# Graph attention stack: the one-head layer's division by the softmax sum, on ScalarE in place of VectorE

## The chip, the cores and the metric

The kernel runs on one core of one Trainium2 chip. The metric is the device time of one execution in microseconds, as the median of several. The core has a matrix engine (TensorE, "PE" in the profile; its weight loads are "PEld"), VectorE ("DVE"), ScalarE ("ACT"), GpSimd ("POOL") and SyncE ("SP", which here only issues DMAs). Each engine works through its own instructions in order; between engines there are semaphores.

## The reference

A stack of four graph attention layers over N = 3327 nodes with 512 features and one sparse 0/1 adjacency matrix (symmetric, with self loops). The layers have 8, 4, 1 and 8 heads. The third, with one head, is the one that matters here:

```
h  = relu(layernorm(x))            # before every layer
h  = h @ W                         # 3327 x 512
e  = leaky_relu(s1[:, None] + s2[None, :], 0.2)      # s1 = h @ a1, s2 = h @ a2
e  = where(adj > 0, e, -9e15)
h' = softmax(e, axis=1) @ h
x  = x + elu(h')
```

The softmax is computed as a sum of exp(e) times rows of h, and a division by the sum of exp(e). That last product of a 128 x 512 tile with one reciprocal per row is what this document calls a mean.

## The kernel before, in words

The nodes are padded to 3328 and cut into 26 tiles of 128 rows, sorted by the number of neighbours. The first layer's preparation turns the adjacency matrix into lists of neighbours. Then a layer treats its tiles in two ways. Tiles with few neighbours (17 of 26 in the third layer) work from lists: `Tile.fetch` gathers a neighbour's row for each of the 128 nodes by an indirect DMA on GpSimd (L834), four neighbours to a group and seven groups ahead; `scored` adds the scores on VectorE (L887, L889) and takes their exponential on ScalarE (L890); `group` multiplies and adds the rows. With one head, `group` does this on VectorE alone: L909 writes the first product into the PSUM tile `bank`, L911 adds the others to it. Tiles with many neighbours (9 in the third layer, in three sets of three) are dense: `Wholes` takes all 26 tiles of rows one after the other, ScalarE makes weights r (L1116), VectorE masks them (em, L1123), TensorE multiplies them with the rows into three PSUM banks `whole` (L1150); GpSimd and VectorE add up the sums (L1136, L1142).

Both sorts run interleaved. The program is written in steps, one group of a list tile to a step, and the order on TensorE, VectorE, ScalarE and GpSimd is that of the program; SP's order is found by a scheduler. Within a step there are places, in this order: "first" (loads, mask product and the next weights, products of the dense tiles), the scores and exponentials of the next step, "scored", the group itself, and "last". A tile's end is spread over later steps by `ends`: `bent` (ScalarE, L944 and L946, for the elu), `added` (VectorE, L952 and L958), `centre` (ScalarE, L966 and L969), `root` (L974 on VectorE, L431 on GpSimd), `turn` (TensorE, L450), `cut` (ScalarE, hT, L457), `project` (TensorE, pv, L468) and `rows` (ScalarE, v, L475, then a DMA to the table of the next layer).

`Tile.finish` puts `divisors` (L926 to L928) and, with one head, `means` (L934) into "last" of the tile's last step. `Wholes.means` (L1161 and L1077 three times) stands three steps after a set's last row tile. In this layer the PSUM pool "o" has one buffer for each name, so the `bank` of the next list tile is the same memory:

```python
            pools = {"o": pool("ps_o", 1 if whole else 2, **psum)}
            ...
                pools.update(w=pool("ps_w", 3, **psum), e=pool("epool", 1))
```

`whole` has three buffers, one for each tile of a set, which the next set takes over. The means are written to SBUF, to parts of `low`: two in turn for list tiles, three for dense ones.

Of the kernel before, what the change touches and what calls it, by code (L numbers as in the profile page):

```python
# [14 lines left out]
AF = mybir.ActivationFunctionType  # L15
OP = mybir.AluOpType
# [779 lines left out]
def tile_gat_lists(ctx: ExitStack, tc: tile.TileContext, x, adj, ws, avs, out, ident, half, slots, L, low, spare, tabx, tabs):  # L796
# [7 lines left out]
    nc = tc.nc  # L804
# [40 lines left out]
    class Tile:  # L845
# [84 lines left out]
        def means(self):  # L930
            H, den = HEADS[self.l], self.den
            if H == 1:
                self.y = next(ys)
                nc.vector.tensor_scalar(self.y, self.po, den[:, 0:1], None, OP.mult)  # L934
                return
            self.y = self.po
            y = self.y.rearrange("p (h d) -> p h d", h=H)
            nc.vector.tensor_tensor(y, y, den[:, :H].unsqueeze(2).to_broadcast([P, H, F // H]), OP.mult)
# [133 lines left out]
    class Whole(Tile):  # L1072


        def means(self):
            self.y = low[:, self.t % 3 * F:(self.t % 3 + 1) * F]
            nc.vector.tensor_scalar(self.y, self.po, self.den, None, OP.mult)  # L1077

    class Wholes:

# [380 lines left out]
```

## Time and profile before

| | us |
|---|---|
| median of 3 executions | 3030.45 |
| lowest, highest | 3009.33, 3045.77 |
| the profiled execution, its own time | 2458.72 |
| its span, first to last instruction | 2456.9 |
| PE busy in it | 2082.3 |
| DVE busy | 1918.9 |
| POOL busy | 1751.1 |
| ACT busy | 911.0 |
| L934, 17 instructions on DVE | 12.8 |
| L1077, 9 instructions on DVE | 6.2 |

The profiled execution is shorter than the others. Times inside it are measured from the start of its span. The third layer's instructions lie between about 1490 and 1930 us. A row of a group of instructions gives line, engine, operation, output and input, shapes, count, then busy time, mean time of one in ns, and the time for which the engine was idle just before these instructions, with what ended that. A line of the timeline gives start, length, engine, line and operation, and in brackets an idle time before it. Instructions of one engine can overlap by some tens of ns, so the time that one keeps its engine is read from start to next start.

### The profile page before, as it was taken

How to read it: one execution, taken by the hardware profiler on the slowest of the kernel's cores; microseconds unless marked ns; L12 is line 12 of the kernel's file. 1: busy time of each engine (PE TensorE's matmuls, PEld its weight loads, DVE VectorE, ACT ScalarE, POOL GpSimd, SP SyncE). 2: the span in 40 equal slices, each digit the busy share in tenths (PEclk: the TensorE clock that was granted, in tenths of full speed). 3: DMA queues.
4: the chain of work that ended last, by engine and by line, in shares of the span. 5: the costliest groups of instructions: out<-in, count | busy, mean ns of one | idle time of the engine just before them, and what ended most of it. 6: DMA issues, size and time to landing. Idle time of an engine off the chain costs nothing. (4 is left out here: it accounts for less than half of the span.)

```text
span 2456.9 us, 26822 instructions
## 1 busy us (share of the span) xinstructions
PE 2082.3 (85%) x6832; PEld 1164.1 (47%) x6832; DVE 1918.9 (78%) x5004; ACT 911.0 (37%) x2506; POOL 1751.1 (71%) x1739
## 2 busy tenths in 40 slices
PE   3788689999998857989999986879696699999897
PEld 1666345455444423545455543445354455455443
DVE  6988787887767736888888865988989488787776
ACT  5877024343331113433333323443333343333330
POOL 7898467777777767776777747676666477777775
PEclk9988899999999988999999997989897899999999
DMA  6886579999988788887888857878776588888885
GB/s 229 320 297 235 173 232 290 291 291 295 278 270 237 229 230 246 263 242 235 247 260 256 253 152 254 252 243 248 217 250 186 165 250 251 242 249 248 242 242 171
DMA packets 262490, 599.55 MB, mean 244 GB/s; under 512 B 103923, under 2 KB 121331, under 8 KB 257974
## 3 DMA queue, kind: packets, MB, share of 16 engines
q0 software_dynamic: 126128, 438.08, 59.5%
q1 hardware_dynamic: 132454, 152.86, 19.3%
q10 hardware_dynamic: 3744, 6.82, 0.8%
q8 instruction: 55, 0.90, 0.1%
q14 instruction: 109, 0.89, 0.1%
HBM read 547.96 MB, written 49.65 MB: 243 GB/s over the span
## 5 line engine op out<-in xcount | busy, mean ns | idle before, releaser
L921 PE MATMUL bank<-m,ident 128*128 128x512 f32 x2608 | 1200.8, 606 | 136.3 <-DVE m L916 135.6
L916 DVE TENSOR_TENSOR m<-g,pw 128x512 f32<-128x512 f32 x1304 | 810.8, 681 | 136.9 <-ACT pw L890 130.3
L834 POOL DMA_INDIRECT g<-tab,idxb x734 | 699.7, 953 | 249.0 <-issue 166.9
L921 PEld LDWEIGHTS bank<-m,ident 128*128 128x128 f32 x2608 | 480.9, 192 | 716.3 <-issue 342.5
L468 PE MATMUL pv<-w,hT 128*128 128x264 f32 x1664 | 436.3, 417 | 66.4 <-ACT hT L457 41.3
L890 ACT ACTIVATE pw<-z 128x32 f32<-128x32 f32 (+4 forms) x362 | 69.8, 193 | 948.8 <-DVE z L889 948.7
L468 PEld LDWEIGHTS pv<-w,hT 128*128 128x128 f32 x1664 | 335.2, 205 | 168.2 <-ACT hT L457 47.5
L834 POOL DMA_INDIRECT g<-tabx,twiceb x342 | 324.2, 948 | 104.8 <-issue 77.1
L834 POOL DMA_INDIRECT g<-tab,idxa x297 | 283.3, 954 | 144.5 <-issue 79.9
L1150 PE MATMUL whole<-ve,em 128*128 128x512 f32 x468 | 230.1, 644 | 45.0 <-DVE em L1123 38.5
L694 POOL TENSOR_TENSOR key<-a,keys 128x3328 int32<-128x3328 int32 (+1 forms) x29 | 189.4, 6536 | 15.9 <-DVE cand L703 11.8
L911 DVE SCALAR_TENSOR_TENSOR bank<-g,L,bank 128x512 f32<-128x512 f32 x243 | 183.2, 754 | 6.8
L887 DVE TENSOR_TENSOR z<-g,pw 128x32 f32<-128x32 f32 (+4 forms) x362 | 63.5, 175 | 149.9 <-DMA g<-tab,idxb 48.2
L1150 PEld LDWEIGHTS whole<-ve,em 128*128 128x128 f32 x468 | 94.0, 206 | 158.2 <-issue 97.1
L834 POOL DMA_INDIRECT g<-tabx,twicea x99 | 94.6, 955 | 69.3 <-issue 32.2
L703 DVE MAX8 cand<-key 128x8 f32<-128x208 int32 x416 | 143.7, 364 | 0.1
L450 PE MATMUL pt<-ident,xn 128*128 128x128 f32 x416 | 67.6, 288 | 50.2 <-ACT hT L457 18.6
L1116 ACT ACTIVATE r<-low,mc,b 128x384 f32<-128x384 f32 x78 | 52.6, 675 | 151.3 <-DVE em L1123 127.8
L1264 ACT ACTIVATE r<-low,spare 128x256 f32<-128x256 f32 x208 | 98.9, 476 | 5.1
L889 DVE SCALAR_TENSOR_TENSOR z<-z 128x32 f32<-128x32 f32 (+5 forms) x434 | 86.1, 198 | 15.1 <-DVE z L887 0.2
L450 PEld LDWEIGHTS pt<-ident,xn 128*128 128x128 f32 x416 | 53.8, 149 | 87.7 <-issue 36.4
L431 POOL TENSOR_TENSOR rstd<-ve,half 128x1 f32<-128x1 f32 x52 | 31.9, 614 | 79.7 <-DVE ve L974 42.5
(180 smaller groups left out, 2161.9 us busy)
## 6 DMA issues: line engine op xcount, KB each, us to landing
a<-in_adj SPq DMA_DIRECT2D x25, 1664.0 KB, 8.5
tab<-v SPq DMA_DIRECT2D x78, 264.0 KB, 3.9
ve<-tab SPq DMA_DIRECT2D x78, 264.0 KB, 3.9
g<-tab SPq DMA_DIRECT2D x66, 264.0 KB, 4.2
tabx<-vx SPq DMA_DIRECT2D x26, 528.0 KB, 5.0
g<-tab,idxb POOLq DMA_INDIRECT x734, 3.9
low<-tab SPq DMA_DIRECT2D x52, 132.0 KB, 3.5
room<-tab SPq DMA_DIRECT2D x52, 132.0 KB, 3.7
```

Of the source, the lines that this page charges most:

```text
L450: nc.tensor.transpose(pt[:, k, :], xn[:, k * P:(k + 1) * P], ident)
L468: nc.tensor.matmul(pv[:, s, :HF + 8], hT[:, k, :], W.w[:, k, s, :], start=(k == 0), stop=(k == KC - 1))
L694: nc.gpsimd.tensor_tensor(key[:, c:c + quarter], a[:, c:c + quarter], keys[:, c:c + quarter], OP.mult)
L703: nc.vector.max(cand[:, g * 8:(g + 1) * 8], key[:, g * SEG:(g + 1) * SEG])
L834: nc.gpsimd.indirect_dma_start(out=out_, out_offset=None, in_=table, in_offset=bass.IndirectOffsetOnAxis(ap=which, axis=0))
L889: nc.vector.scalar_tensor_tensor(z, z, SLOPE, z, OP.mult, OP.max)
L890: nc.scalar.activation(self.wt[:, k0:k0 + n, :H], z, AF.Exp)
L911: nc.vector.scalar_tensor_tensor(acc, v, w, acc, OP.mult, OP.add)
L916: nc.vector.tensor_tensor(m[:, q, :].rearrange("p (s h d) -> p s h d", s=2, d=D), v.rearrange("p s (h d) -> p s h d", d=D), wt[:, k0 + q, ...
L921: nc.tensor.matmul(self.po, ident, m[:, q, :], start=(k0 + q == 0), stop=(k0 + q == K - 1))
L1150: nc.tensor.matmul(tl.po.rearrange("p (s m) -> p s m", s=2), e[:, q * P:(q + 1) * P], v.rearrange("p (s m) -> p s m", s=2)[:, :, :F // 2], ...
L1264: nc.scalar.activation(self.r[:, h, :], self.a[:, g, :], AF.Relu, bias=-1.0, scale=self.b[:, j, g:g + 1])
```

## The change

The means of the third layer are computed by ScalarE, as an activation of the kind Copy with the reciprocal as its per-row scale, in place of a `tensor_scalar` multiplication on VectorE. This is done for the list tiles (L934) and for the dense tiles (L1077). Place in the program, inputs and outputs are the same.

```diff
@@ Tile.means
             H, den = HEADS[self.l], self.den
             if H == 1:
                 self.y = next(ys)
-                nc.vector.tensor_scalar(self.y, self.po, den[:, 0:1], None, OP.mult)
+                nc.scalar.activation(self.y, self.po, AF.Copy, scale=den[:, 0:1])
                 return
@@ Whole.means
         def means(self):
             self.y = low[:, self.t % 3 * F:(self.t % 3 + 1) * F]
-            nc.vector.tensor_scalar(self.y, self.po, self.den, None, OP.mult)
+            nc.scalar.activation(self.y, self.po, AF.Copy, scale=self.den)
```

## The prediction

> **What bounds the kernel now.** I read the page's engine totals first, then the third layer alone, since only it runs the changed lines: their 26 instructions start between 1504.9 and 1913.0 us.
>
> ```profile
> PE 2082.3 (85%) x6832; PEld 1164.1 (47%) x6832; DVE 1918.9 (78%) x5004; ACT 911.0 (37%) x2506; POOL 1751.1 (71%) x1739
> ```
>
> No engine bounds the whole. The busy times by stretch (length, then PE, PEld, DVE, ACT, POOL, TensorE clock, DMA share, GB/s) say who bounds where:
>
> ```profile
> 1490.00:1930.00 440.00, 353.08 (x1035) 200.30 (x1035) 366.62 (x728) 170.04 (x409) 283.76 (x300) 0.89 0.74 226
> 1530.00:1640.00 110.00, 91.73 (x252) 48.59 (x250) 101.64 (x199) 49.52 (x136) 78.97 (x84) 0.91 0.82 251
> 1650.00:1675.00 25.00, 24.44 (x82) 16.12 (x83) 13.32 (x25) 7.79 (x16) 13.82 (x15) 0.93 0.73 216
> 1770.00:1845.00 75.00, 74.60 (x228) 42.20 (x226) 61.99 (x123) 29.69 (x61) 49.52 (x52) 0.97 0.78 242
> 1848.00:1900.00 52.00, 32.68 (x98) 21.47 (x98) 48.04 (x105) 19.60 (x44) 33.68 (x36) 0.74 0.62 178
> ```
>
> VectorE (DVE) is 92% busy in 1530 to 1640 and in 1848 to 1900; TensorE is full in 1650 to 1675 and 1770 to 1845. ScalarE (ACT) is 39% busy over the layer. Third, the chain that ended last, for the stretch between:
>
> ```profile
> 1702.82 0.76 DVE low L934
> 1703.64 0.95 POOL g L834
> ...
> 1716.25 0.99 POOL g L834
> 1717.55 4.01 DMA g<-tab,idxb
> 1722.55 0.68 DVE bank L911
> ```
>
> Here the chain runs over GpSimd's queue of gathers: VectorE ends a mean, but what it next lacks at 1722 is a gathered row. So a saving on VectorE counts in two stretches of about 160 us, and elsewhere only so far as it lets TensorE or GpSimd begin sooner.
>
> **What the Trainium skill says.** "ScalarE: Activation LUTs", *Table sets*, says that copy is in every set, so no table load is added; the trace agrees, one load of 1.3 us in the whole program beside many Copy, Relu and Exp. "VectorE: DVE Perf Modes", *Why PSUM operands drop a tier*, says that fp32 with a PSUM operand runs at the basic rate; the trace has 751 ns for the 512 columns, so VectorE gives up no fast form. "PSUM — Partial Sum Buffer", *Engine vs sequencer instructions*, says that the ScalarE and VectorE queues are strict first in, first out; the trace agrees where a ScalarE step stands 3.01 us for TensorE and ScalarE's later steps start after it (shown below). So a mean on ScalarE stands behind whatever is ahead of it there.
>
> **The change, part by part.** Rows of the groups by shape (count, busy us, mean ns, idle before):
>
> ```profile
> L475 ACT ACTIVATE v<-pv,rstd 128x528 f32<-128x528 f32 x26 | 18.0, 691 | 38.4 <-issue 20.7 <-PE pv L468 16.0 <-POOL parts L1136 1.7
> L934 DVE TENSOR_SCALAR low<-bank,den 128x512 f32<-128x512 f32 x17 | 12.8, 751 | 0.6
> L1077 DVE TENSOR_SCALAR low<-whole,den 128x512 f32<-128x512 f32 x9 | 6.2, 745 | 0.1
> ```
>
> *Removed from VectorE:* 17 means at L934 and 9 at L1077. One blocks the engine from its start to the next start, 0.67 us in the lines below (1504.90 to 1505.57), less than the 751 ns because the next overlaps its end. The limit of the gain is 26 x 0.67 = 17.4 us.
>
> *Added to ScalarE:* the same 26 as Copy with a per-partition scale out of PSUM. The nearest row is L475, the same form at 528 columns: 691 ns. The skill's ScalarE page (*What ACT_TABLE_LOAD costs*) gives 186 + 93 for the pointer + 0.833 x 512 = 706 ns as an estimate. Bounds 0.60 (L457, no pointer, PSUM) and 0.71; I take 0.69. 18 us more on an engine with 270 us idle in this layer costs nothing by itself.
>
> *The added wait.* A tile's running sum "bank" has one buffer. Until now VectorE read it and then overwrote it in its own order; now L909, the next tile's first product, has to wait for ScalarE's read, and all of VectorE stands behind L909. What covers it:
>
> ```profile
> 1504.70 0.17 DVE L928 RECIPROCAL den<-den 128x1 f32<-128x1 f32 x1
> 1504.90 0.75 DVE L934 TENSOR_SCALAR low<-bank,den 128x512 f32<-128x512 f32 x1
> 1505.57 0.61 DVE L1123 SCALAR_TENSOR_TENSOR em<-r,c,mk 128x384 f32<-128x384 f32 x1
> 1506.09 0.15 DVE L887 TENSOR_TENSOR z<-g,L 128x4 f32<-128x4 f32 x1
> 1506.28 0.21 DVE L889 SCALAR_TENSOR_TENSOR z<-z 128x4 f32<-128x4 f32 x1
> 1506.41 0.74 DVE L909 TENSOR_SCALAR bank<-g,L 128x512 f32<-128x512 f32 x1
> ```
>
> Between mean and L909 lie a mask product and the scores, 0.84 us (1505.57 to 1506.41). ScalarE needs 0.03 to start (such hand-overs are 0.02 to 0.04 us in the chain), 0.69, and 0.02 back: 0.74. So with ScalarE free the wait is covered and 0.67 is gained whole. If that cover is gone, as at 1894.28 where only 0.28 us of scores lie between, the wait is 0.43 and 0.24 is left of the gain.
>
> ScalarE is not always free. Behind the mean stand the weights r (L1116) for the next mask product and the scores' exponentials; ahead of it can stand steps that wait for TensorE:
>
> ```profile
> 1647.27 0.60 ACT L457 ACTIVATE hT<-pt 128x512 f32<-128x512 f32 x1 [3.01 <-PE pv L468]
> ```
>
> The reciprocal of that tile ends at 1646.15, so the mean would run 1647.8 to 1648.5 and push r, now at 1647.76, back by 0.6 us. By the order of instructions the same happens at 1781.1 (v and hT ahead until 1782.5), and at 1597.3 a target row and an exponential are ahead until 1598.06, which leaves no gain.
>
> The sum along the layer, in the profiled execution:
> - To 1616. The gain at 1504 goes into VectorE's 4.77 us wait for a partial sum at 1515.8. Then 0.67 at 1531, 0.5 at 1551 (two mask products, the second follows r), 0.67 at 1576, 0 at 1597: 1.8 us.
> - At 1616 the second group of three dense tiles needs its PSUM banks: TensorE waits for the first mean, whose length hardly differs. The 2 us that VectorE saves on three means fall ahead of TensorE's stretch to 1675: 0. The push at 1647 delays its start by 0.6: 1.2 us left.
> - 1679 gives 0.67 to GpSimd's root and queue; 1703 and 1726 go into the gather chain: 1.9. 1746 gives 0.67 ahead of the third dense group: 2.5. The three means at 1753 go into waits for a gather at 1757 and for TensorE, full to 1845; so do 1781, 1813 and 1840.
> - 1848 to 1900: 0.67 at 1865, 3 x 0.66 at 1877 (no L909 behind them), 0.24 at 1894: 2.9, in all 5.4.
> - The tail. The last tile's mean stands behind two v on ScalarE, and the chain there is
>
> ```profile
> 1914.44 0.70 ACT v L475
> 1915.14 0.53 ACT neg L944
> ```
>
> so 0.6 us come in ahead of L944: plus 0.6.
>
> Sum: 4.8 us. The built order also moves about 20 mask loads ahead of a row load on the SP queue, past nothing else of weight. A mask product waits 4.13 us for loads at 1844.6, so this is worth between 0 and 4 us of gain, or as much loss if a row load comes late; I take 0. Orders on TensorE and GpSimd are unchanged.
>
> The profiled execution took 2458.72 us, 2456.9 of it span. The three times shown are 3009 to 3046, 23% longer, for a reason that the profile doesn't show. Against the profiled time the sum is 2453.9; carried over as it is, or in proportion (x 1.23, 5.9 us), the median of 3030.45 becomes 3024 to 3026. I take **3025**.
>
> **Rivals.**
> *The whole gain.* VectorE's share of 83% over the layer is the highest, and its waits may shrink with it: 25 means x 0.67 less 0.6 is 16.2 us, 20 in proportion: 3010 to 3014. Against it: TensorE is full for 100 us and GpSimd's gathers carry the chain at 1703 to 1722.
> *Nothing.* If the longer time outside the profile comes from TensorE or the transfers, VectorE bounds less there, and its gain ends in waits for them: 3030.
> *Slower, ScalarE stuck behind TensorE.* The mean stands behind hT or v, which wait 3.0 to 5.65 us for TensorE at 1647, 1656, 1671 and 1803, and L909 with all of VectorE waits too, which starves TensorE of mask products. At a wait of 3 us past the reciprocal a tile end costs 3 - 0.67 = 2.3; at 14 of 16 that is 33 us: 3063. It decides from the point where ScalarE comes free more than some 0.8 us (the cover) after the reciprocal. In the trace that holds at two of 17 tile ends (1646, 1781), so it needs a much slower TensorE.
> The change does what it says: the 26 instructions leave VectorE's order and stand in ScalarE's.
>
> **How the numbers follow.** Likeliest, 2 to 10 us gained: 0.52. Nothing within 2 us: 0.25. Whole gain, 10 to 21: 0.12. Slower: 0.11. A change of under about 1% (30 us) can hardly be told from none here, as the three times themselves spread by 36 us. A median of three such times moves by some 12 to 16 us, so the range runs from the whole gain's 3013 less 12 to 3030 plus 16: 3001 to 3046. Over 1% faster needs the whole gain and scatter: 0.07. Over 1% slower needs most of the slower rival: 0.07. Within: 0.86.
>
> **What would show it.** In the profile after: 26 Copy rows at L934 and L1077 on ACT near 690 ns; VectorE's busy time in the layer lower by 19 us; a new wait at L909 for ScalarE, under 0.5 us at most tile ends; the layer shorter by about 5 us. Waits of over 1 us at L909 at most tile ends would show the slower rival; an unshortened layer with as much more idle time on VectorE, the second. A layer shorter by over 12 us would prove wrong the claim that TensorE and gathers absorb most of it.

## The result, and the profile after

| | before | after |
|---|---|---|
| median of 20 executions each, us | 3024.24 | 3008.55 |
| lowest, highest | 3005.93, 3045.77 | 2986.96, 3038.47 |
| ratio, with its 95% interval | | 0.9943 (0.9922 to 0.9964) |

The changed kernel is faster by 17 us (11 to 24). That is 0.6%, so within the 1% to which the prediction gave 0.86, and 3008.55 lies in its range of 3001 to 3046. The sum behind the forecast, 4.8 us, is too small: 17 is three and a half times as much.

An execution of this program takes about 2460 us or about 3030 us, whichever of the two kernels it is; each comparison of times below is between runs on one chip, and profiles of the two lengths are set side by side only for single steps and busy times.

The engine totals of the changed kernel, in its profile of 3010.3 us of span (own time 3012.32):

```profile
PE 2242.4 (74%) x6832; PEld 1224.4 (41%) x6832; DVE 1895.9 (63%) x4978; ACT 929.7 (31%) x2532; POOL 1750.4 (58%) x1739
```

Against the page of before, DVE has 26 instructions and 23 us of busy time less, ACT 26 and 19 us more. The changed lines by shape, in the stretch of the third layer of the same profile (count, busy us, mean ns, idle before):

```profile
L909 DVE TENSOR_SCALAR bank<-g,L 128x512 f32<-128x512 f32 x17 | 12.7, 750 | 3.4 <-issue 1.6 <-ACT L L890 1.5 <-ACT low L934 0.4
L934 ACT ACTIVATE low<-bank,den 128x512 f32<-128x512 f32 x17 | 11.7, 686 | 21.6 <-DVE den L928 9.2 <-DVE bank L911 4.3 <-DVE parts L1142 3.9
L1077 ACT ACTIVATE low<-whole,den 128x512 f32<-128x512 f32 x9 | 5.5, 685 | 3.6 <-issue 2.0 <-DVE bank L911 1.5
```

A mean on ScalarE costs what was predicted, 685 to 686 ns against the 690 that the prediction took (it also had an estimate of 706). The new wait at L909 for ScalarE is 0.4 us in all.

Both kernels were profiled again on one chip of the shorter kind, spans 2462.8 and 2451.1 us. The third layer there, from its second mask product to the start of the last activation at L1240 (length, then PE, PEld, DVE, ACT, POOL, TensorE clock, DMA share, GB/s); first before:

```profile
1495.10:1938.10 443.00, 354.60 (x1050) 201.90 (x1050) 366.87 (x728) 171.00 (x413) 286.47 (x303) 0.89 0.74 225
```

and after:

```profile
1492.80:1927.40 434.60, 349.13 (x1050) 200.70 (x1050) 346.61 (x702) 186.75 (x440) 286.10 (x304) 0.90 0.75 230
```

VectorE lost 20.3 us of busy time and the layer 8.4 us, so VectorE's idle time in it rose from 76.1 to 88.0 us. The two spans differ by 11.7 us. Besides the 8.4, 2.3 us arise ahead of this stretch, in the first two layers, which run no changed line, and 1.0 after it. Executions differ by that much without the change: the layer's first reciprocal starts at 1504.70 in the profile of before and at 1510.00 in e1, which is the same kernel.

### The profile page after: what moved, and what is told of

Its sections match the earlier page's. It is cut to its first block, busy times and chain, and to the rows that moved or that the text cites. A ratio compares the mean times of both kernels' runs of the same rounds, so it can differ in the third digit from the quotient of the medians.

```text
span 3010.3 us, 26823 instructions
## 1 busy us (share of the span) xinstructions
PE 2242.4 (74%) x6832; PEld 1224.4 (41%) x6832; DVE 1895.9 (63%) x4978; ACT 929.7 (31%) x2532; POOL 1750.4 (58%) x1739
## 4 chain that ended last, share of the span: by engine, by line
PE 26%; DVE 12%; issue 12%; another core or an unknown queue 7%; ACT 5%; POOL 4%; DMA 2%; SPq 1%; DVEq 0%; POOLq 0%; ACTq 0%
PE bank L921 17%; DVE m L916 5%; PE pv L468 4%; POOL g L834 3%; PE whole L1298 3%; DVE bank L911 2%; PE whole L1150 2%; DMA g<-tab,idxb 1%; DVE x L958 1%; DVE z L887 1%; ACT r L1264 1%; DVE z L889 1%; ACT spare L1275 0%; ACT pw L890 0%
## 5 line engine op out<-in xcount | busy, mean ns | idle before, releaser
L921 PE MATMUL bank<-m,ident 128*128 128x512 f32 x2608 | 1331.4, 658 | 379.9 <-DVE m L916 218.3
L921 PEld LDWEIGHTS bank<-m,ident 128*128 128x128 f32 x2608 | 529.1, 211 | 1046.3 <-issue 643.8
L911 DVE SCALAR_TENSOR_TENSOR bank<-g,L,bank 128x512 f32<-128x512 f32 x243 | 183.3, 754 | 11.5 <-issue 3.6
L475 ACT ACTIVATE v<-pv,rstd 128x528 f32<-128x528 f32 x78 | 54.1, 694 | 327.2 <-remote 194.3
L1275 ACT ACTIVATE spare<-room,low 128x64 f32<-128x64 f32 x208 | 58.2, 337 | 179.1 <-remote 73.6
L889 DVE SCALAR_TENSOR_TENSOR z<-z 128x32 f32<-128x32 f32 (+5 forms) x434 | 80.1, 185 | 30.4 <-issue 8.1
```

Source lines behind the costliest of these rows:

```text
L889: nc.vector.scalar_tensor_tensor(z, z, SLOPE, z, OP.mult, OP.max)
L911: nc.vector.scalar_tensor_tensor(acc, v, w, acc, OP.mult, OP.add)
L921: nc.tensor.matmul(self.po, ident, m[:, q, :], start=(k0 + q == 0), stop=(k0 + q == K - 1))
```

## The experiments

All were timed in five rounds, with 5 to 22 executions of each kernel. The first four ran on a chip of the shorter kind (before: 2461.98 us), the next four on one of the longer (before: 3040.23), the last two on such a chip in another call (before: 3042.45). The last column is the ratio's, not the difference of the two medians. The theory: the gain is VectorE's time, and more of it comes through than the sum allowed, because TensorE's full stretches pass a saving on. Its rivals: the gain is something else that comes with the edit (the order of loads, the place of the means), or, as the prediction had it, the first two dense sets give nothing. In the expectations, theory W stands for every moved mean giving its 0.67 us, theory P for the prediction's sum.

| label | edit | us | ratio (95%) | against before, us |
|---|---|---|---|---|
| e1_before_again | none | 2464.59 | 1.0005 (0.9996 to 1.0015) | +1 (-1 to +4) |
| e2_after_again | both lines on ScalarE | 2449.93 | 0.9950 (0.9936 to 0.9964) | -12 (-16 to -9) |
| e3_list_only | L934 alone | 2453.64 | 0.9965 (0.9952 to 0.9978) | -8.6 (-12 to -5) |
| e4_dense_only | L1077 alone | 2456.32 | 0.9975 (0.9968 to 0.9982) | -6.2 (-7.9 to -4.4) |
| f1_extra_dve | before, VectorE's time added | 3047.66 | 1.0024 (1.0002 to 1.0046) | +7.3 (+0.6 to +14) |
| f2_time_given_back | after, the same time added | 3039.56 | 0.9999 (0.9972 to 1.0025) | 0 (-8.5 to +7.6) |
| f3_mean_ahead | after, list means earlier | 3032.12 | 0.9968 (0.9947 to 0.9990) | -10 (-16 to -3) |
| f4_after_third | both lines on ScalarE | 3031.60 | 0.9960 (0.9938 to 0.9982) | -12 (-19 to -5) |
| g1_first_two_sets | L1077, first six dense tiles | 3036.52 | 0.9975 (0.9953 to 0.9997) | -7.6 (-14 to -1) |
| g2_third_set | L1077, last three | 3042.41 | 1.0006 (0.9983 to 1.0030) | +2 (-5 to +9) |

**Both kernels again.** Before, unchanged, and after, unchanged.

> The kernel before, unchanged, beside itself: what a difference of nothing looks like (within 0.3%, 9 us), and a profile of it of the length that the other executions have (about 3020 us). Theory W (VectorE bounds the whole third layer, so each moved mean gives its 0.67 us): the third layer, from its first mask product to its last mean, takes about 17 us more here than in the changed kernel's profile. Theory P (the prediction's sum: TensorE and the gathers absorb most of it): about 5 us more, and the other 10 us of the measured 16 lie outside the third layer.

> The changed kernel, a second profile and a second comparison. Both theories: 0.2 to 0.8% faster (6 to 24 us), as measured. It says how far two profiles of one kernel differ by stretches of the program.

The gain is there again, 12 us, and stands well clear of the 1 us by which the unchanged kernel differs from itself. The later run on the other kind of chip gives 12 as well. So nothing shows that the longer time, 23%, which the prediction could not explain, makes the gain larger; the intervals (9 to 16 and 5 to 19) are too wide to rule it out. Between the profiles of e1 and e2 the third layer differs by the 8.4 us above, halfway between theory P's 5 and theory W's 17. e1 was expected at about 3020 us and ran at 2465.

> The changed kernel a third time, for its profile: whether the TensorE clock is halved near 1645 us again, right behind the start of the second dense group, as in two of the profiles with the list means moved. If it is tied to the change, it is there; if it is chance, it need not be. Time as before: 12 us faster than the kernel before (9 to 16).

**One line at a time.** Either the list means (L934) or the dense means (L1077) go to ScalarE.

```diff
 # e3_list_only
-                nc.vector.tensor_scalar(self.y, self.po, den[:, 0:1], None, OP.mult)
+                nc.scalar.activation(self.y, self.po, AF.Copy, scale=den[:, 0:1])
 # e4_dense_only
-            nc.vector.tensor_scalar(self.y, self.po, self.den, None, OP.mult)
+            nc.scalar.activation(self.y, self.po, AF.Copy, scale=self.den)
```

> Only the 17 means of the list tiles move to ScalarE; the 9 of the dense tiles stay on VectorE. Theory W: 16 x 0.67 less 0.6 at the tail, 10 us faster (0.33%). Theory P: about 2 us faster (1.9 by 1746, 0.9 after 1848, less 0.6), not to be told from none.

> Only the 9 means of the dense tiles move. Theory W: 9 x 0.66, 6 us faster (0.2%). Theory P: 2 us faster, from the third set alone.

Both lines gain. By the prediction's own terms, the list tiles would give 2.8 us (1.8, three times 0.67, 0.24, less two times 0.6) and the dense ones 2.0. Measured are 8.6 and 6.2. The dense ones give, within their interval, all of the 9 x 0.67 = 6.0 us that they take from VectorE. The list tiles are off by more than the dense ones.

**Which dense sets.** The prediction had 0 for the first two sets and all of the dense gain in the third.

```diff
 # g1_first_two_sets; g2_third_set has "self.t >= 6"
-            nc.vector.tensor_scalar(self.y, self.po, self.den, None, OP.mult)
+            if self.t < 6:
+                nc.scalar.activation(self.y, self.po, AF.Copy, scale=self.den)
+            else:
+                nc.vector.tensor_scalar(self.y, self.po, self.den, None, OP.mult)
```

> Only the six means of the first two dense sets (at 1616 and 1753 us of the profile before) move to ScalarE. The prediction's sum put both at nothing, because TensorE's full stretches follow: 0. If a saving ahead of a full stretch passes through it, because the stretch begins sooner: 6 x 0.66 = 4 us faster (0.15%), and in the profile 2 us at each set that stay until the layer's end.

> Only the three means of the third dense set (at 1877 us) move. The prediction's sum and theory W agree: 2 us faster (0.08%), seen in the profile between 1877 and 1894 us and kept to the layer's end.

The first two sets gain, 7.6 us with zero outside the interval. That is more than six means can give (4 us), but the interval, 1 to 14, holds the 4. So the zeros of the prediction were wrong. For the third set the interval is too wide to tell its 2 us from none; the traces below show them.

**VectorE's time, given back and added.** After each mean, VectorE also computes x + x of the tile's 128 x 512 rows into a part of an SBUF tile that nothing reads: added work, on top of the whole computation. In one run this is put into the kernel before, in the other into the kernel after.

```diff
+    def scr():
+        return L[:, F:2 * F]
...
+                nc.vector.scalar_tensor_tensor(scr(), xs[self.t], 1.0, xs[self.t], OP.mult, OP.add)
...
+            nc.vector.scalar_tensor_tensor(scr(), xs[self.t], 1.0, xs[self.t], OP.mult, OP.add)
```

> The kernel before, with one more VectorE instruction behind each of the 26 means: an addition of 128x512 out of SBUF into unused SBUF, some 0.65 us each, 17 us in all. Nothing waits for its result. It measures the worth of VectorE's time at these places by itself. Theory W (VectorE's time counts in full): 17 us slower (0.7%). Theory P (only the stretches of the prediction's sum): about 5 us slower (0.2%). From the 12 us that the change gained on this chip: 10 to 14.

> The changed kernel, with the same VectorE addition behind each mean: the means are on ScalarE, but VectorE has its 0.65 us to spend all the same. If VectorE's time is the whole cause, the gain of 12 us goes to zero or below: 0 to 4 us slower than the kernel before (the cost of the added wait, of r pushed back and of the tail). If the gain came from the order of the loads, or from the means ending sooner, it stays: 8 to 12 us faster.

What one such addition costs VectorE is read from start to start on its timeline, in f1_extra_dve (line numbers are 4 or 5 higher there):

```profile
2318.14 0.75 DVE L1081 TENSOR_SCALAR low<-whole,den 128x512 f32<-128x512 f32 x1
2318.81 0.68 DVE L1082 SCALAR_TENSOR_TENSOR L<-x 128x512 f32<-128x512 f32 x1
2319.41 0.74 DVE L1081 TENSOR_SCALAR low<-whole,den 128x512 f32<-128x512 f32 x1
```

The mean takes 0.67 us (2318.14 to 2318.81), the addition 0.60 (to 2319.41), 26 of them 15.6 us. With them in the changed kernel, where all means are still on ScalarE, the gain is gone: 0. In the kernel before they cost 7.3 us, less than the 10 to 14 expected, though the interval (0.6 to 14) holds these and theory P's 5 as well. So the gain falls away with 15.6 us of VectorE while ScalarE's part stays, which rules out the place of the means by itself (the intervals of f2 and f4 share only -8.5 to -5). The scale is 12 of 17.4 us, about 0.7 us for each us taken away, and 7.3 of 15.6 for each added, with wide intervals.

The order of loads did not stay: the scheduler builds it anew for every kernel. Of the 657 DMA issues on SP's queue, compared in order by the names of their tiles, 34 stand in another place in the changed kernel than in the one before. In f2_time_given_back only 8 do, and 26 differ from the changed kernel; in f1_extra_dve 28 differ from before. So these two runs alone cannot tell VectorE's time from the order of loads. The traces can. If the new order helped, some wait would be shorter. Instruction by instruction on VectorE, from the layer's first reciprocal to its last, e2 is 9.6 us ahead of e1. Of this, 18.5 us arise at the steps right behind the reciprocals, where the means stood, and 1.7 by other steps that are shorter in sum. Waits that are longer take back 11.2, and waits that are shorter give 0.6 in all. So the order of loads gives no part of the gain that could be seen here.

**The mean ahead of hT.** In the changed kernel the mean of a list tile could stand behind hT on ScalarE; here reciprocal and mean are the first things in "last".

```diff
+            if HEADS[self.l] == 1:
+                at.setdefault((s, "last"), [])[:0] = [self.divisors, self.means]
+            else:
+                later(s, "last", self.divisors)
+                later(a, "last", self.means)
```

> The changed kernel, with reciprocals and mean of a list tile moved to the front of the step's last place, so that on ScalarE the mean stands ahead of hT, which waits for TensorE. If the mean held up behind hT costs what the profile of the changed kernel showed near 1650 us (about 4 us of VectorE's and TensorE's time), this is 14 to 16 us faster than before, 2 to 4 more than the change. If that was chance of the TensorE clock, it is as fast as the change: 12 us.

Measured is -10 against -12 of the changed kernel in the same call: no difference that can be told, which is the case in which the profile's loss near 1650 us was chance. The single place that it aimed at did change, as shown below, but it is worth 0.6 us. None of these versions beats the changed kernel.

## Why the prediction was right and wrong

The price of a mean on ScalarE, the cover and the direction were right, and the size was too small, because terms were put at nothing that came through. That the median lay in the range says little: the range was 45 us wide for the scatter of medians, and of the 21.9 us between 3030.45 and 3008.55, 6.2 are the median of before itself, which moved when 20 executions stood in place of 3.

**Where the lag grows.** The table follows the reciprocals ahead of the means through the layer: by how much each comes sooner (minus) or later than in e1_before_again, counted from the layer's first reciprocal. Places are named by the prediction's times, the profile of before; the predicted column is the running sum of its steps at that point.

| place | predicted | list alone (e3) | dense alone (e4) | both (e2) |
|---|---|---|---|---|
| 1597 | -1.8 | -2.4 | -0.5 | -0.4 |
| 1616, dense set | -1.8 | -3.2 | -0.6 | -1.1 |
| 1619, behind its means | -1.8 | -3.2 | -2.7 | -3.2 |
| 1646 | -1.8 | -4.8 | -3.6 | -3.6 |
| 1679 | -1.2 | 0.0 | -5.2 | +1.2 |
| 1746 | -1.9 | -1.6 | -5.2 | -0.3 |
| 1753, dense set | -2.5 | -2.3 | -5.2 | -1.0 |
| 1781 | -2.5 | -3.8 | -8.1 | -3.9 |
| 1840 | -2.5 | -3.6 | -9.1 | -4.9 |
| 1877, dense set | -3.2 | -5.6 | -9.1 | -7.2 |
| 1894 | -5.2 | -5.6 | -11.2 | -9.4 |

These are single executions, so a step of one column is a place and not a time of the kernel; the timed medians are those of the table above. Where a mean is taken away, the next step moves up by 0.70 to 0.79 us at a list tile and by 2.10 at a dense set, somewhat more than the 0.67 and 3 x 0.66 of the prediction, since it also starts 0.08 us behind the reciprocal, and the mean started 0.20 behind it.

Two things move the columns by as much without a mean: TensorE's clock, and VectorE steps that are drawn out (both are shown below).

**The price and the cover: right.** ScalarE takes 687 ns in e2 as well, and the hand-over is covered. Groups by shape of e2_after_again in the layer:

```profile
L1123 DVE SCALAR_TENSOR_TENSOR em<-r,c,mk 128x384 f32<-128x384 f32 x78 | 47.9, 614 | 37.7 <-ACT r L1116 32.3 <-POOL parts L1136 5.4
L909 DVE TENSOR_SCALAR bank<-g,L 128x512 f32<-128x512 f32 x17 | 12.7, 750 | 2.0 <-ACT low L934 2.0
L934 ACT ACTIVATE low<-bank,den 128x512 f32<-128x512 f32 x17 | 11.7, 687 | 22.6 <-DVE den L928 22.6
```

L909 waits for ScalarE for 2.0 us over the whole layer, at 3 of 17 tile ends. This also refutes the slower rival, for which the prediction named over 1 us at most of them. A covered tile end on VectorE's timeline in that profile:

```profile
1534.82 0.16 DVE L928 RECIPROCAL den<-den 128x1 f32<-128x1 f32 x1
1534.89 0.62 DVE L1123 SCALAR_TENSOR_TENSOR em<-r,c,mk 128x384 f32<-128x384 f32 x1
1535.43 0.16 DVE L887 TENSOR_TENSOR z<-g,L 128x4 f32<-128x4 f32 x1
1535.62 0.17 DVE L889 SCALAR_TENSOR_TENSOR z<-z 128x4 f32<-128x4 f32 x1
1535.73 0.75 DVE L909 TENSOR_SCALAR bank<-g,L 128x512 f32<-128x512 f32 x1
```

and the mean on ScalarE's:

```profile
1535.01 0.69 ACT L934 ACTIVATE low<-bank,den 128x512 f32<-128x512 f32 x1 [2.81 <-DVE den L928]
```

ScalarE's mean ends at 1535.70 and L909 starts at 1535.73: 0.84 us after the mask product's start, as in the profile of before.

**The tile ends up to 1597: not settled.** List alone has -2.4, both -0.4, predicted -1.8. Half a us of the difference is there at 1531. The rest comes at 1543, where the z of a list group is drawn out in e1 and e2 but not in e3; in e1, e2 and e3:

```profile
1543.36 1.54 DVE L889 SCALAR_TENSOR_TENSOR z<-z 128x4 f32<-128x4 f32 x1
1541.14 1.67 DVE L889 SCALAR_TENSOR_TENSOR z<-z 128x4 f32<-128x4 f32 x1
1542.70 0.17 DVE L889 SCALAR_TENSOR_TENSOR z<-z 128x4 f32<-128x4 f32 x1
```

So 1.4 of the 2.4 us of list alone are not the means'. At 1551 the second mask product waits for r 0.80 us in e1, 1.49 in e3 and 2.51 in e2, because r stands behind b (L1112), which in e2 waits for a row load until 1556.5.

**"The 2 us that VectorE saves on three means fall ahead of TensorE's stretch to 1675: 0" is the step that failed.** The lag at 1619 exceeds that at 1616 by 2.1 us in both columns that move these means, and by none in the column that doesn't. Until 1646 it does not shrink. The reason given was that TensorE is full afterwards. But what TensorE works on in the full stretch are mask products that VectorE makes; when these come 2 us sooner, the stretch can begin and end sooner. Of the two savings inside the later stretch (1781 and 1813), 1.0 of some 1.5 us came through in e2 and none in e3.

**The same at 1753: "go into waits for a gather at 1757 and for TensorE".** VectorE's timeline at the second set, first in e1_before_again:

```profile
1757.65 0.17 DVE L1161 RECIPROCAL den<-pt 128x3 f32<-128x3 f32 x1
1757.86 2.07 DVE L1077 TENSOR_SCALAR low<-whole,den 128x512 f32<-128x512 f32 x3
1759.84 0.68 DVE L952 SCALAR_TENSOR_TENSOR low<-ex,low 128x512 f32<-128x512 f32 x1
...
1762.08 1.69 DVE L889 SCALAR_TENSOR_TENSOR z<-z 128x4 f32<-128x4 f32 x1
```

and in e4_dense_only:

```profile
1753.51 0.17 DVE L1161 RECIPROCAL den<-pt 128x3 f32<-128x3 f32 x1
1753.60 0.66 DVE L952 SCALAR_TENSOR_TENSOR low<-ex,low 128x512 f32<-128x512 f32 x1
```

From the reciprocal to L952 it is 2.19 us before and 0.09 after. No wait takes the 2.1 us. Where the prediction read the end of a wait for a gather, VectorE has no idle time; what is long there is the z (1.69 us in e1, 1.68 at 1757.00 in the profile of before), a step of VectorE's own that is drawn out. It is not drawn out in e4, where a later step is instead:

```profile
1755.82 0.17 DVE L889 SCALAR_TENSOR_TENSOR z<-z 128x4 f32<-128x4 f32 x1
1758.93 1.50 DVE L952 SCALAR_TENSOR_TENSOR low<-ex,low 128x512 f32<-128x512 f32 x1
```

nor in e3, where the dense means have not moved:

```profile
1760.09 0.17 DVE L889 SCALAR_TENSOR_TENSOR z<-z 128x4 f32<-128x4 f32 x1
```

So the lag at 1781 exceeds that at 1753 by 2.8 us in both columns that move these means: 2.1 from the means, 1.5 from z, less 0.8 for the longer L952. In the list column it grows by the 1.5 of z alone. TensorE then waits for less. Its timeline in e1, the transposes ahead of the full stretch:

```profile
1774.20 1.12 PE L450 MATMUL pt<-ident,xn 128*128 128x128 f32 x4 [5.17 <-ACT hT L457]
```

and in e4:

```profile
1767.22 0.84 PE L450 MATMUL pt<-ident,xn 128*128 128x128 f32 x4 [2.94 <-ACT hT L457]
```

and in e3:

```profile
1770.69 1.11 PE L450 MATMUL pt<-ident,xn 128*128 128x128 f32 x4 [4.14 <-ACT hT L457]
```

So 2.2 us of TensorE's own idle time ahead of the stretch are gone in e4; 1.0 of it is gone in e3 too, where only z is shorter. The timing of the first two sets alone, 7.6 us, says without a trace that they are not 0.

**Zeros of the list tiles came through as well.** The table shows them in both columns that move the list means: 0.7 to 0.8 us behind 1597 (predicted 0), 1.5 from 1679 to 1746 (predicted 0.7), and 2.0 to 2.3 from 1840 to 1877 (predicted 0.7; part of it a drawn-out z that is short again). These are the means at 1597, 1726 and 1840, some 0.75 each. The mean at 1619 has no term in the sum and gave 0.8 in e3; in e2 a wait for ScalarE took it. With the first two dense sets (4.2), these (2.2) and that one, the 4.8 becomes an estimate of 12 us, from single profiles. That is near the timed 12; the list tiles alone come to 5.8 of their 8.6 (5 to 12), and the rest of those stays open.

**The third set: right.** From 1877 to 1894 the lag grows by 2.1 us in e4 and 2.1 in e2, predicted 2.0. The timing of this set alone cannot confirm it.

**The pushes: right in size.** At 1647 the prediction had 0.6 us for the mean between hT and r. ScalarE's timeline in f4_after_third:

```profile
2083.42 0.60 ACT L457 ACTIVATE hT<-pt 128x512 f32<-128x512 f32 x1 [3.03 <-PE pv L468]
2083.92 0.68 ACT L934 ACTIVATE low<-bank,den 128x512 f32<-128x512 f32 x1
```

and TensorE's:

```profile
2077.09 2.74 PE L1150 MATMUL whole<-ve,em 128*128 128x512 f32 x6
2079.66 3.72 PE L468 MATMUL pv<-w,hT 128*128 128x264 f32 x16
...
2087.30 2.95 PE L468 MATMUL pv<-w,hT 128*128 128x264 f32 x7 [3.91 <-ACT v L475]
```

TensorE's idle time ahead of the next pv is 3.91 us there and 3.33 in e1: 0.58. In f3_mean_ahead the mean runs while hT still waits, and it is 3.33 again. ScalarE there:

```profile
2059.27 0.69 ACT L934 ACTIVATE low<-bank,den 128x512 f32<-128x512 f32 x1 [1.00 <-issue]
2063.00 0.60 ACT L457 ACTIVATE hT<-pt 128x512 f32<-128x512 f32 x1 [3.04 <-PE pv L468]
```

The tail costs 0.7 us, predicted 0.6. ScalarE at the last tile of e2:

```profile
1908.15 0.70 ACT L475 ACTIVATE v<-pv,rstd 128x528 f32<-128x528 f32 x1 [3.97 <-PE pv L468]
1908.74 0.68 ACT L934 ACTIVATE low<-bank,den 128x512 f32<-128x512 f32 x1
1909.46 0.63 ACT L944 ACTIVATE neg<-low 128x512 f32<-128x512 f32 x1
```

**Most of what the profiles of e2 and e3 lose at 1646 to 1679 is not the change.** Both columns with the list means fall back by 4.8 us there, far more than the push. In both profiles TensorE's clock fell to half in this place. Stretches of 10 us at the same work, e1:

```profile
1645.20:1655.20 10.00, 6.79 (x26) 4.49 (x26) 8.62 (x23) 4.57 (x11) 8.13 (x9) 1.00 0.70 214
```

and e2:

```profile
1640.00:1650.00 10.00, 9.78 (x26) 5.81 (x26) 6.02 (x17) 2.27 (x7) 8.09 (x10) 0.69 0.66 186
```

The same 26 matrix instructions take 9.78 us of TensorE in place of 6.79, at a mean clock of 0.69. TensorE's line for six products in e2:

```profile
1640.98 5.31 PE L1150 MATMUL whole<-ve,em 128*128 128x512 f32 x6
```

In f4, shown above, the same changed lines have 2.74 us, and so has e1; in f3 they have 4.44. In g1_first_two_sets, where the list means are on VectorE, the six products are slow too:

```profile
2065.31 3.83 PE L1153 MATMUL whole<-ve,em 128*128 128x512 f32 x6
```

The drop therefore comes and goes between executions, with and without the list means on ScalarE. The 1.7 us that the dense column gains at 1646 to 1679 are the clock as well, for e1 was slow there itself. The same 16 products pv, in e1 and in e4:

```profile
1655.60 5.51 PE L468 MATMUL pv<-w,hT 128*128 128x264 f32 x16 [3.33 <-ACT v L475]
1653.15 3.83 PE L468 MATMUL pv<-w,hT 128*128 128x264 f32 x16 [3.33 <-ACT v L475]
```

The drop fits the Trainium skill, "TensorE: Matmul & The Clock Gate", *What's actually happening*: the clock is halved after an idle window of about 3.4 us, and the windows run freely, so that where they fall changes from run to run. In slices of 1 us, e2's clock is 0.66 from 1639, 0.50 from 1640 to 1646 and 0.93 from 1646: 3.41 us of full clock missing, which is 6.8 us at half speed, two such windows. The 3.4 us ahead of the drop (1636 to 1639.4) were not wholly idle: TensorE was busy for 1.15 of them.

**The rivals and the range.** "Nothing" (0.25) is out by every timing of the changed kernel. "The whole gain" (0.12) had 16 to 20 us, within limits of 10 to 21: all three medians of the changed kernel, 17 and twice 12, lie within these limits and outside the likeliest case's 2 to 10 (0.52), though the intervals of the 12s (9 to 16 and 5 to 19) reach into it. A part of the 17.4 us is absorbed all the same: VectorE's idle time in the layer is up by 11.9 us in e2. Instruction by instruction, 6.4 us of its longer waits there are for r, 2.0 at L909 for the mean, and 1.2 for the exponential of the elu (L946); the clock's drop at 1646 to 1679 stands behind the greater part of the first and the last. The claim that TensorE and the gathers absorb most of it falls by the timings: about two thirds come through. (The single pair of profiles, with 8.4 us, stays under the 12 that the prediction had named for this.) Carrying one profile's sum over to the median did no harm: the gain is about the same 12 us on both kinds of chip.

## What to carry to other kernels

A saving just ahead of a full stretch of another engine need not be hidden by it, and here it was not: ask what lets the stretch begin before writing the saving off. When a busy engine's step goes to an idler one, look first at what stands ahead of it in the new queue and whether the reader of the freed buffer has other work in between; here 0.84 us of it covered a step of 0.69. To settle whether an engine's time is the cause, give the same time back to it in the changed kernel: that costs one extra instruction. Then look at what else the build moved; here the order of loads went back nearly to that of the kernel before, and only the waits in the traces could rule it out.

## What the runs showed of the hardware beyond that

A small VectorE step was drawn out tenfold where it met an addition of GpSimd. The z of 1.69 us in e1 runs from 1762.08 to 1763.77, beside GpSimd's addition of mask products (both inputs in SBUF):

```profile
1762.72 1.02 POOL L1136 TENSOR_TENSOR parts<-em 128x384 f32<-128x384 f32 x1
```

It ends at 1763.74. In the third layer of the profiles e1 to e4, L889 runs 288 times. In 13 of them it takes 1.51 to 1.69 us in place of 0.17: these 13 overlap an addition at L1136 and end 0.03 to 0.04 us after it, and none of the other 275 overlaps one. L952 is drawn out 24 times, always beside such an addition. The Trainium skill, "SBUF — State Buffer", *Who interferes with whom*, says that a VectorE instruction with two SBUF inputs contends with a GpSimd instruction that reads SBUF, that the ports they share are an exclusive lock, and that the order of issue decides who waits. The traces agree: z and L952 have two SBUF inputs, while L911 and L1123, which have one input in PSUM, overlap L1136 118 and 58 times and are never drawn out. But in the record each of these 13 z starts ahead of the addition, by 0.47 to 0.64 us, and z is the one that is held. Which steps meet an addition changed as VectorE shifted, and this moves the columns above by 0.7 to 1.5 us at places without a mean.

TensorE's half clock in one place (9.78 us of work in place of 6.79) moved single profiles by 3 us and more in a layer of 440. That is over half of the sum that was predicted, so a step of this size is to be read from what stands ahead of and behind it, and its worth from timed rounds.
